# When the parts of a sequence may be added: a rule by slots, and an output bias added at the norm

## The chip, the cores and the metric

The kernel runs on one core of a Trainium2 chip. The metric is the device time of one execution in microseconds (us); a kernel's time is the median of its runs. Beside the times there is one profiled execution of each kernel, with a trace of every engine: TensorE (PE, with its weight loads as PEld), VectorE (DVE), ScalarE (ACT), GpSimd (POOL) and SyncE (SP), which here issues all plain DMAs.

## The reference: what is computed

The input x holds 16 sequences of 512 tokens with 256 features, all float32. Each token is normalised (mean and variance over its features); from the normalised tokens xn come three parts, and their sum with x is the output:

```
xn  = layernorm(x)
out = x + attention(xn) + routed(xn) + shared(xn)
attention: q, k, v = xn Wq' + bq, ...; 16 heads of 16; causal, window of 128 keys
           softmax + 1e-9, times v, then  @ Wo' + bo
routed:    logits = xn gate'; the 2 best of 8 experts (beta added for the choice),
           weight sigmoid(logit); expert: (silu(xn Wg) * (xn Wu)) Wd, width 512
shared:    one more expert of the same form for every token
```

bo is the output bias that the change moves: one vector of 256, the same for every token.

## The kernel before

**Stages.** A sequence is four tiles of 128 tokens. `norm` normalises sequences in groups of three: it loads x into the tiles `x_in` (`load_x`, two buffers per place, the next group loaded ahead), forms statistics (L211, L215) and the reciprocal root (L222 to L227) on VectorE, writes xn (L233) to memory as `xn_d`, turns it with TensorE and stores `xT_d` (L249), and makes the values v (stored as `v_d`) and the router's logits. `lane_sums` (L279, L281) adds up the values of a sequence on GpSimd, and `sum_values` (L289, L292) turns these sums with a matmul. The first sequence is normalised ahead of everything, from the tile `x_first`, the others in the background. `route` then sorts all tokens by expert. `experts` runs 135 blocks of 128 tokens, and writes their results with an indirect DMA to `y_d`. `early` is the shared expert of one sequence: it loads xT (L800), makes the hidden values (`gate_up`, L764) and adds the second product to the sum (`add_down`, L789, L794).

**Sums.** Every sequence has a running sum of 512 KB. Each of its three parts (attention, routed, shared) loads it into a tile `acc` with `load_sums`, adds its own and stores it with `store_sums` (L827), in any order but one at a time (`in_work`). The first part to come loads x itself and adds bo to it on GpSimd (L815, L816), the next load what is in memory as `acc_d` (L813), and the last part stores to the output. Attention adds its product with Wo at L777 and L780 (`output`), the routed part multiplies the two results of each token by their weights (L968) and adds them (L972) on GpSimd, in two halves per sequence, each with a y tile loaded at L990.

**Order.** The program is written out by hand in slots. The generator `attention` yields four times per step, 20 steps per sequence, 1304 slots in all. In each slot the main loop may advance the background (norms, then the router), advances the filling at an even pace (shared parts as long as the router isn't done, then all expert blocks, then the shared parts that are left), and advances the endings (routed parts, from when the last expert block is out). `now[0]` is the sequence whose attention runs. A sequence's attention is added two groups after its last scores, in slot 80 b + 101 or so. What is written out this way sets priorities: a planner with its own costs and times then puts each engine's instructions in order, and may let one go ahead of earlier ones that wait in its reckoning. On each engine and queue the order is then fixed.

**What the change touches.** `free(b)` says whether a shared or routed part of sequence b may start: nobody else is at its sum, and its attention is either not yet under way (b above `now[0]`) or has been added. `endings` takes from the free sequences those above `now[0]` first, then the lowest; `filling` takes those above `now[0]` first, and the highest.

Of the kernel before, what the change touches and what calls it, by code (L numbers as in the profile page):

```python
# [12 lines left out]
ALU = mybir.AluOpType  # L13
AX = mybir.AxisListType

B, S, D = 16, 512, 256
# [3 lines left out]
P = 128  # L20
NT = S // P
# [20 lines left out]
def block_kernel(ctx: ExitStack, tc: tile.TileContext, a: dict, out: bass.AP):  # L42
    nc = tc.nc
# [27 lines left out]
    acc_d = dram.tile([TT * P, D], FP, tag="acc_d", name="acc_d")  # L71
    y_d = dram.tile([2 * TT * P + P, D], FP, tag="y_d", name="y_d")
    by_tile = lambda d, b: d[b * S : (b + 1) * S].rearrange("(t p) d -> p t d", p=P)
# [22 lines left out]
    x_first = part_tile(0, "x_in").rearrange("p (t d) -> p t d", d=D)  # L96
# [104 lines left out]

    logits = const.tile([P, TT, E], FP, tag="logits", name="logits")

    def norm(xs, first=None):

        n = len(xs) * NT
        st = two.tile([P, NG * NT, 6], FP, tag="st", name="st")
        mv = two.tile([P, NG * NT, 2], FP, tag="mv", name="mv")
        for i, x_sb in enumerate(xs.values()):
            for t in range(NT):  # L210
                nc.vector.bn_stats(st[:, i * NT + t], x_sb[:, t])  # L211
                if t % 2:
                    yield
        for i in range(n):
            nc.vector.bn_aggr(mv[:, i], st[:, i])  # L215
        yield
        small = lambda name: two.tile([P, NG * NT], FP, tag=name, name=name)[:, :n]
        var, root, rstd, yy = small("var"), small("root"), small("rstd"), small("yy")
        nc.vector.tensor_scalar_add(var, mv[:, :n, 1], EPS)
        nc.scalar.activation(root, var, AF.Sqrt)  # L220
        yield
        nc.vector.reciprocal(rstd, root)  # L222

        nc.vector.tensor_mul(yy, rstd, rstd)
        nc.vector.tensor_mul(yy, yy, var)
        nc.vector.tensor_scalar(yy, yy, -0.5, 1.5, ALU.mult, ALU.add)
        nc.vector.tensor_mul(rstd, rstd, yy)  # L227
        yield
        for i, (b, x_sb) in enumerate(xs.items()):
            xn = two.tile([P, NT, D], FP, tag="xn", name="xn")  # L230
            for t in range(NT):
                j = i * NT + t
                nc.vector.tensor_scalar(  # L233
                    xn[:, t], x_sb[:, t], mv[:, j, 0:1], rstd[:, j : j + 1],
                    ALU.subtract, ALU.mult,
                )
                if t % 2:
                    yield
            nc.sync.dma_start(out=by_tile(xn_d, b), in_=xn)
            tag = "xT" if first else "hr"  # L240
            xT = two.tile([P, KC, S], FP, tag=tag, name="xT_new")
            for c in range(KC):
                tp = bank_a()
                for t in range(NT):
                    nc.tensor.transpose(tp[:, ts(t, P)], xn[:, t, ts(c, P)], ident)
                nc.scalar.copy(xT[:, c], tp)
            if first:
                first(xT)
            nc.sync.dma_start(out=xT_d[b], in_=xT)  # L249
            yield  # L250
            v = four.tile([P, NT, D], FP, tag="acc", name="v_new")
            for t in range(NT):
                pv = bank_b()
                for c in range(KC):
                    nc.tensor.matmul(  # L255
                        pv[:, : D + E], lhsT=xT[:, c, ts(t, P)], rhs=wv[:, c],
                        start=c == 0, stop=c == KC - 1,
                    )
                nc.vector.tensor_tensor(v[:, t], pv[:, :D], bv, ALU.add)
                nc.scalar.copy(logits[:, b * NT + t], pv[:, D : D + E])  # L260
                if t % 2:
                    yield
            nc.sync.dma_start(out=v_d[b].rearrange("(t p) n -> p t n", p=P), in_=v)
            if first:
                load_values(ws[b])
                first_xT[b] = xT
            lane_sums(v)
            yield
            if not first:
                sum_values(b)  # L270
            normed.add(b)

    vall = const.tile([P, B, KC], FP, tag="vall", name="vall")
# [9 lines left out]
    def sum_values(b):  # L283

        pall = bank_b()
        for c in range(KC):

            rows = one.tile([P, 2, QD, DK], FP, tag=f"vsum{c}", name="vsum_c")
            nc.gpsimd.tensor_copy(  # L289
                rows, vsum.rearrange("p (g c s d) -> p c s g d", c=2, s=2, d=DK)[:, c]  # L290
            )
            nc.tensor.matmul(  # L292
                pall[:, c : c + 1], lhsT=rows.rearrange("p s g d -> p (s g d)"),
                rhs=ones[:, 0:1], start=True, stop=True,
            )
        nc.scalar.mul(vall[:, b], pall[:, :KC], EVERY)
# [509 lines left out]
    in_work = set()  # L806

    def load_sums(b):
        assert b not in in_work
        in_work.add(b)  # L810
        acc = four.tile([P, NT, D], FP, tag="acc", name="acc")
        if parts_of[b]:
            nc.sync.dma_start(out=acc, in_=by_tile(acc_d, b))  # L813
            return acc
        nc.sync.dma_start(out=acc, in_=by_tile(a["x"].rearrange("b s d -> (b s) d"), b))  # L815
        nc.gpsimd.tensor_tensor(  # L816
            acc, acc, bo.unsqueeze(1).to_broadcast([P, NT, D]), ALU.add
        )
        return acc

    out_rows = out.rearrange("b s d -> (b s) d")
# [4 lines left out]
        to = out_rows if len(parts_of[b]) == 3 else acc_d  # L826
        nc.sync.dma_start(out=by_tile(to, b), in_=acc)  # L827

    def free(b):

        return b not in in_work and (b > now[0] or "attention" in parts_of[b])

    def early(b):

# [126 lines left out]
    def endings():  # L961
        added = []

        def add():
            b, half, acc, y = added.pop()
            tiles = slice(NT // 2 * half, NT // 2 * (half + 1))
            weight = prob[:, :, b * NT : (b + 1) * NT][:, :, tiles].rearrange("p k t -> p t k")
            nc.gpsimd.tensor_tensor(  # L968
                y, y, weight.unsqueeze(3).to_broadcast([P, NT // 2, 2, D]), ALU.mult
            )  # L970
            for k in range(2):
                nc.gpsimd.tensor_tensor(acc[:, tiles], acc[:, tiles], y[:, :, k], ALU.add)  # L972
            if half:
                store_sums(b, acc, "routed")

        left = set(range(B))
        while left or added:
            ready = [b for b in left if free(b)] if all_routed else []
            if not ready:
                if added:  # L980
                    add()
                yield
                continue
            b = min(ready, key=lambda b: (b <= now[0], b))
            left.remove(b)
            acc = load_sums(b)
            for half in range(2):
                y = two.tile([P, NT // 2, 2, D], FP, tag="xn", name="y_in")
                r0 = 2 * P * (b * NT + NT // 2 * half)
                nc.sync.dma_start(  # L990
                    out=y.rearrange("p t k d -> p t (k d)"),
                    in_=y_d[r0 : r0 + P * NT].rearrange("(t p k) d -> p t (k d)", p=P, k=2),
                )
                yield
                yield
                if added:
                    add()
                added.append((b, half, acc, y))
                yield
                yield  # L1000
# [7 lines left out]
    def filling():  # L1008


        b = 0
        while not routed:
            while b not in normed:
                yield None
            yield from early(b)
            b += 1
        yield from experts()
        all_routed.append(True)
        rest = set(range(b, B))
        while rest:  # L1020
            ready = [b for b in rest if free(b)]
            if not ready:
                yield None
                continue
            b = max(ready, key=lambda b: (b > now[0], b))
            rest.discard(b)
            yield from early(b)

    all_routed, now = [], [0]

    def test_maxima():

# [14 lines left out]

    for _ in norm({0: x_first}, first_projections):
        pass
    routed = []  # L1050
    behind, fill, ends = background(), filling(), endings()
    slots_in_all = 4 * (B * STEPS + len(STEP_BLOCKS) + 1)
    pace, owed = (NB * 6 + B * 24) / (slots_in_all - 4), 0.0
    for n, now[0] in enumerate(attention()):
        if not routed and n % 8 in (0, 2, 4, 6, 7):
            if next(behind, routed) is routed:
                routed.append(True)
        owed += pace
        while owed >= 1:
            owed -= 1  # L1060
            next(fill, None)
        next(ends, None)
        if n == 8:
            sum_values(0)
        if n == 4 * (B * STEPS + 1):
            again = test_maxima()
# [68 lines left out]
```

## Time and profile before

| | |
|---|---|
| median of 3 runs | 1988.27 us (1985.82 to 1989.53) |
| the profiled execution | 1989.47 us |
| its span, first to last instruction | 1987.8 us |
| mean granted clock of TensorE | 0.983 |
| busy: PE, DVE, ACT, POOL | 1916.6, 1211.1, 684.6, 605.8 us |
| DMA | 386.58 MB, mean 194 GB/s |

Times in the views are counted from the start of the span. A row of a timeline or of the chain of waits begins with its start and its length in us, then the engine, the line of the kernel and the tiles (output<-input); "SPq" is SyncE's queue, whose length is the time to issue. A row of groups gives the number of instructions, their busy time and mean length in ns, and the idle time of the engine ahead of them with what ended it. In the chain, "issue" is time in which an engine waited for nothing that the profile shows. The 40 digits of the page give the busy share of an engine in tenths, one for each fortieth of the span (49.7 us).

### The profile page before, as it was taken

The page shows a single profiled execution, that of the slowest core. Times are in us where ns is not written, and L with a number is a line of the kernel's source. Part 1 is how long each engine was busy: PE and PEld are TensorE (multiplying, and loading weights), DVE is VectorE, ACT ScalarE, POOL GpSimd, SP SyncE. Part 2 cuts the span into 40 slices and gives each one's busy share as a digit, 9 for nine tenths or more (in the row PEclk, how much of TensorE's full clock was granted, in tenths as well). Part 3 has the DMA queues.
Part 4 walks back from the last instruction along what each step waited for, and adds up shares of the span by engine and source line. Part 5 has one row for each costly group of instructions (what it writes and reads, how often), then busy time and mean ns, then how long its engine had stood idle before and what let it go on. Part 6 is the DMA issues. An engine that isn't in the chain of part 4 may idle for free.

```text
span 1987.8 us, 35311 instructions
## 1 busy us (share of the span) xinstructions
PE 1916.6 (96%) x12011; PEld 1654.5 (83%) x12011; DVE 1211.1 (61%) x3912; ACT 684.6 (34%) x1752; POOL 605.8 (30%) x765
## 2 busy tenths in 40 slices
PE   7899999999899999999999999999999999998985
PEld 4677767767789999999989899998989899985763
DVE  5767756599945565555555566555655565555652
ACT  3333323321133333333333333333333333332320
POOL 5212212210022222222222323222222222228884
PEclk9899999999999999999999999999999999999997
DMA  7634434341257676777676777777676777757774
GB/s 198 196 120 154 151 88 133 128 124 35 59 183 245 204 233 229 223 243 220 208 235 219 223 234 232 218 251 212 217 226 216 225 235 233 217 182 215 228 238 147
DMA packets 355773, 386.58 MB, mean 194 GB/s; under 512 B 118528, under 2 KB 262976, under 8 KB 355584
## 3 DMA queue, kind: packets, MB, share of 16 engines
q1 hardware_dynamic: 342624, 348.82, 55.9%
q0 software_dynamic: 12960, 35.41, 5.5%
q8 instruction: 98, 1.61, 0.3%
q14 instruction: 91, 0.75, 0.1%
HBM read 307.67 MB, written 68.09 MB: 189 GB/s over the span
## 4 chain that ended last, share of the span: by engine, by line
PE 88%; DVE 8%; POOL 1%; DMA 1%; issue 1%; ACT 0%; SPq 0%; POOLq 0%; DVEq 0%; ACTq 0%
PE a L897 24%; PE a L557 13%; PE b L915 12%; PE c L605 12%; PE a L764 9%; PE b L789 5%; PE b L777 3%; PE b L255 3%; PE a L524 2%; PE a L514 2%; PE b L887 2%; DVE hot_b L448 1%; DVE den L622 1%; DVE hot_l L444 1%; DVE probs L546 1%
## 5 line engine op out<-in xcount | busy, mean ns | idle before, releaser
L897 PE MATMUL a<-xgT,w 128*128 128x128 f32 x4320 | 548.7, 276 | 1.9 <-DVE maxima L546 1.0
L897 PEld LDWEIGHTS a<-xgT,w 128*128 128x128 f32 x4320 | 526.9, 193 | 12.7 <-issue 8.5
L550 ACT ACTIVATE probs<-probs,maxima 128x160 f32<-128x160 f32 (+4 forms) x1024 | 346.2, 401 | 528.8 <-DVE maxima L546 508.4
L546 DVE CUSTOM_DVE_ANT_0 probs<-a,window 128x160 f32<-128x160 f32 (+4 forms) x1024 | 254.1, 297 | 235.4 <-PE a L557 225.0
L605 PEld LDWEIGHTS c<-turned,spread_v 128*128 128x128 f32 x2048 | 308.9, 191 | 58.2 <-issue 42.6
L605 PE MATMUL c<-turned,spread_v 128*128 128x160 f32 (+4 forms) x2048 | 338.1, 290 | 10.5 <-DVE ctxT L623 10.1
L557 PE MATMUL a<-kT,spread 128*128 128x160 f32 (+4 forms) x2048 | 323.2, 295 | 0.0
L557 PEld LDWEIGHTS a<-kT,spread 128*128 128x128 f32 x2048 | 290.4, 192 | 33.2 <-issue 25.0
L877 POOL DMA_INDIRECT xg<-xn_d,source x135 | 132.9, 984 | 472.3 <-PE b L887 416.6
L915 PE MATMUL b<-w,hr 128*128 128x256 f32 x1080 | 271.7, 381 | 0.0
L622 DVE RECIPROCAL den<-den 64x512 f32<-64x512 f32 x64 | 214.1, 3346 | 85.3 <-ACT den L617 82.7
L764 PE MATMUL a<-xT,shared 128*128 128x512 f32 x480 | 242.0, 609 | 11.5 <-DMA xT<-xT_d 11.5
L596 DVE STREAM_TRANSPOSE turned<-probs 128x480 f32<-128x480 f32 (+1 forms) x256 | 161.8, 632 | 104.9 <-ACT probs L550 101.5
L502 POOL COPY spread_v<-v 32x256 f32<-32x256 f32 x256 | 101.4, 397 | 373.8 <-PE c L605 219.9
L922 POOL DMA_INDIRECT y_d<-y,target x135 | 132.4, 981 | 266.3 <-ACT y L921 236.5
L915 PEld LDWEIGHTS b<-w,hr 128*128 128x128 f32 x1080 | 189.8, 190 | 19.6 <-issue 2.6
L753 DVE SCALAR_TENSOR_TENSOR hr<-hr,a 128x512 f32<-128x512 f32 x135 | 91.8, 680 | 136.4 <-ACT hr L752 127.8
L789 PE MATMUL b<-shared,h 128*128 128x256 f32 x512 | 133.1, 392 | 4.4 <-DVE acc L794 2.8
L752 ACT ACTIVATE hr<-a 128x512 f32<-128x512 f32 x135 | 79.9, 592 | 149.5 <-PE a L897 142.2
L764 PEld LDWEIGHTS a<-xT,shared 128*128 128x128 f32 x480 | 83.8, 195 | 50.7 <-issue 36.1
L754 DVE SCALAR_TENSOR_TENSOR hr<-hr,a 128x512 f32<-128x512 f32 x135 | 91.8, 680 | 45.9 <-PE a L897 43.0
L789 PEld LDWEIGHTS b<-shared,h 128*128 128x128 f32 x512 | 94.4, 196 | 20.0 <-DVE acc L794 3.5
(141 smaller groups left out, 1701.1 us busy)
## 6 DMA issues: line engine op xcount, KB each, us to landing
w<-in_gp SPq DMA_DIRECT2D x135, 512.0 KB
w<-in_up SPq DMA_DIRECT2D x135, 512.0 KB
w<-in_dp SPq DMA_DIRECT2D x135, 512.0 KB
acc_d<-acc SPq DMA_DIRECT2D x32, 512.0 KB
acc<-acc_d SPq DMA_DIRECT2D x32, 512.0 KB
y_in<-y_d SPq DMA_DIRECT2D x32, 512.0 KB
xT<-xT_d SPq DMA_DIRECT2D x30, 512.0 KB
xn_d<-xn SPq DMA_DIRECT2D x16, 512.0 KB
```

Of the source, the lines that this page charges most:

```text
L546: nc.vector.tensor_tensor_reduce(out=to, in0=ps, in1=window[:, WIN - n :], scale=-SCALE, scalar=-MASKED, op0=ALU.add, op1=ALU.min, accum_o ...
L550: nc.scalar.activation(to, to, AF.Exp, bias=least, scale=-1.0)
L557: nc.tensor.matmul(ps, lhsT=spreads[group % 2][:, u].rearrange("p g q -> p (g q)"), rhs=w["kT"][:, group // 2, f:e], start=True, stop=True,)
L596: nc.vector.transpose(moved(pT, Q * blocks[0] + P * first, [[WIN, n], [P, SEEN], [1, Q]]), moved(pr, 0, [[WIN, n], [Q, SEEN], [1, Q]]),)
L605: nc.tensor.matmul(av[:, Q * k : Q * k + n], lhsT=spread_v[s][:, k], rhs=pT[:, WIN * k : WIN * k + n], start=k == ORDER[0], stop=k == ORDE ...
L622: nc.vector.reciprocal(den[mine], den[mine])
L764: nc.tensor.matmul(ps, lhsT=wt[:, c, ts(m, P)], rhs=xT[:, c], start=c == 0, stop=c == KC - 1,)
L789: nc.tensor.matmul(po[t][:, :D], lhsT=h[m][:, ts(t, P)], rhs=wd[:, m], start=m == 0, stop=m == MC - 1,)
L877: nc.gpsimd.indirect_dma_start(out=g, out_offset=None, in_=xn_d, in_offset=bass.IndirectOffsetOnAxis(ap=source[:, i : i + 1], axis=0),)
L897: nc.tensor.matmul(hidden[i][which][:, ts(m, P)], lhsT=weights[i, which][:, c, ts(m, P)], rhs=turned[i][:, c], start=c == 0, stop=c == KC - 1,
L915: nc.tensor.matmul(po[:, :D], lhsT=made[i][:, ts(m, P)], rhs=weights[i, 2][:, m], start=m == 0, stop=m == MC - 1,)
L922: nc.gpsimd.indirect_dma_start(out=y_d, out_offset=bass.IndirectOffsetOnAxis(ap=target[:, i : i + 1], axis=0), in_=y, in_offset=None,)
```

## The change

The bias is no longer added by the first part. `add_bias` adds it in place to the x tile of each sequence once its xn has been written, and the tile is stored to `acc_d` at the end of that sequence's norm. `load_sums` always loads from `acc_d`. For the first sequence both stand between its norm and the main loop. `free` no longer looks at `now[0]`: a part may start if the sequence's attention has been added, or if the present slot, plus 20 for a routed part or 40 for a shared one, lies ahead of the slot in which attention is added. The endings take sequences without their attention first.

```diff
+    def add_bias(x_sb):
+        nc.gpsimd.tensor_tensor(x_sb, x_sb, bo.unsqueeze(1).to_broadcast([P, NT, D]), ALU.add)
...
     def norm(xs, first=None):
...
             nc.sync.dma_start(out=by_tile(xn_d, b), in_=xn)
+            if not first:
+                add_bias(x_sb)
...
             if not first:
                 sum_values(b)
+                nc.sync.dma_start(out=by_tile(acc_d, b), in_=x_sb)
             normed.add(b)
...
         acc = four.tile([P, NT, D], FP, tag="acc", name="acc")
-        if parts_of[b]:
-            nc.sync.dma_start(out=acc, in_=by_tile(acc_d, b))
-            return acc
-        nc.sync.dma_start(out=acc, in_=by_tile(a["x"].rearrange("b s d -> (b s) d"), b))
-        nc.gpsimd.tensor_tensor(
-            acc, acc, bo.unsqueeze(1).to_broadcast([P, NT, D]), ALU.add
-        )
+        nc.sync.dma_start(out=acc, in_=by_tile(acc_d, b))
         return acc
...
-    def free(b):
-        return b not in in_work and (b > now[0] or "attention" in parts_of[b])
+    def free(b, slots):
+        added = 4 * ((b + 1) * STEPS + len(STEP_BLOCKS))
+        return b not in in_work and ("attention" in parts_of[b] or clock[0] + slots < added)
...
-            ready = [b for b in left if free(b)] if all_routed else []
+            ready = [b for b in left if free(b, 20)] if all_routed else []
...
-            b = min(ready, key=lambda b: (b <= now[0], b))
+            b = min(ready, key=lambda b: ("attention" in parts_of[b], b))
...
-            ready = [b for b in rest if free(b)]
+            ready = [b for b in rest if free(b, 40)]
...
     for _ in norm({0: x_first}, first_projections):
         pass
+    add_bias(x_first)
+    nc.sync.dma_start(out=by_tile(acc_d, 0), in_=x_first)
...
     for n, now[0] in enumerate(attention()):
+        clock[0] = n
```

More of the change, by code (lines that the diff above doesn't have):

```diff
@@ L1027, in filling @@
             yield from early(b)
-    all_routed, now = [], [0]
+    all_routed, now, clock = [], [0], [0]
     def test_maxima():
```

## The prediction

> **What bounds the kernel now.** I read the page first: the share of each engine and the 40 slices.
>
> ```profile
> span 1987.8 us, 35311 instructions
> PE 1916.6 (96%) x12011; PEld 1654.5 (83%) x12011; DVE 1211.1 (61%) x3912; ACT 684.6 (34%) x1752; POOL 605.8 (30%) x765
> ...
> PE   7899999999899999999999999999999999998985
> ...
> POOL 5212212210022222222222323222222222228884
> ```
>
> TensorE is busy from end to end, so work on other engines is worth something only where the PE row drops: at the start, and in the last slices, where GpSimd (POOL) rises to 8. The windows view gives PE 299.5 of 300 us busy from 1000 to 1300 us, but 74.7 of 80 from 1770, 44.3 of 50 from 1850 and 63.9 of 88 from 1900. Nothing that the change touches in the long middle can move the end; the start and the tail can.
>
> Second, the chain of waits for the tail, from 1955 us on:
>
> ```profile
> 1961.37 0.43 DVE acc L794
> ...
> 1963.33 4.57 PE b L777 x12
> ...
> 1967.92 0.10 DVE acc L780
> 1968.02 8.14 issue
> 1976.17 3.02 POOL acc L972 x3
> ...
> 1979.82 1.26 POOL acc L972
> ```
>
> The last matmul (L777, attention's output of sequence 15) ends at 1967.9. Then 8.14 us pass in which no engine works, and GpSimd adds the routed results of sequence 15. SyncE's timeline says what the 8.14 us are:
>
> ```profile
> 1961.82 0.47 SPq L827 DMA_DIRECT2D out<-acc  x1
> 1968.38 0.37 SPq L827 DMA_DIRECT2D acc_d<-acc  x1
> 1972.11 0.37 SPq L813 DMA_DIRECT2D acc<-acc_d  x1
> 1981.11 0.38 SPq L827 DMA_DIRECT2D out<-acc  x1
> ```
>
> The sum of sequence 15 goes to acc_d (3.73 us until the next DMA may read it), comes back (4.06 us until L972 starts at 1976.17), takes 4 adds (4.92 us) and is stored at 1981.11; 6.7 us later the span ends. The two y tiles were already weighted (L968, until 1968.0), so nothing else holds the end.
>
> Third, the same view at the start, and GpSimd's bias add by form:
>
> ```profile
> 22.95 0.68 POOL vsum L279
> ...
> 25.29 0.30 POOL vsum_c L289
> 25.59 0.04 issue
> 25.64 0.61 PE b L292 x4
> 26.25 0.75 PE a L557 x6
> ```
>
> ```profile
> L816 POOL TENSOR_TENSOR acc<-acc,bo 128x1024 f32<-128x1024 f32 x16 | 37.7, 2355 | 24.1 <-DMA acc<-in_x 15.3 <-issue 8.1
> ```
>
> Until 25.6 us the chain runs through GpSimd: fills, then vsum and vsum_c, which the first PE work after the projections (L292) waits for, with the first scores (L557) behind it.
>
> **Part by part. Which part comes last.** I counted slots through the loops: 1304 slots, 24 steps of filling per shared part, 8 slots per routed part, the experts done at slot 1170. Before, sequences 14 and 15 wait for their attention (slots 1221 and 1301), so the routed part of 15 starts at 1302 and must follow attention 15 through acc_d. After, 14 is let in at 1170 and 15 at 1202 (the limits are 1200 and 1280). But the shared part of 11, in both versions the last of the filling, holds 11 from slot 1274 to 1301, so the routed part of 11 becomes the last one. The round trip is not removed: it now follows the shared part of 11 and lies beside attention 15, whose sum goes straight to the output.
>
> Its length from the rows above: the shared part's last add (L794) ends at 1961.8; store 3.7 gives 1965.5; load 4.1 gives 1969.6; 4 adds of 4.9 give 1974.5, against 1981.1: a gain of 6.6 us. What is late next is attention 15: its store leaves at 1968.4, and with the same 6.7 us behind it would end the span at 1975.1, earlier than 1974.5 + 6.7 = 1981.2, so it is covered. The lower bound: if the load of 11 or its second y tile is queued on SyncE behind attention 15's output store, it leaves at 1968.8, lands at 1972.9, and the adds end at 1977.8: a gain of 3.3. I take 6.4, near the upper end, since the load depends only on a store issued 6.6 us before that output store, and let 0.2 go for its issue.
>
> **Bias at the norm.** 16 adds on GpSimd before, 16 after, at 2.355 us: no change in sum. Fifteen follow the writing of xn; one, for sequence 0, stands ahead of the first scores. The fifteen lie under PE work: from 120 to 420 us PE is busy 296.6 of 300 us. What is queued behind such an add is spread_v (L502) and vsum. Taken out of the tail is one add (at 1854.5); GpSimd then waits 4.56 us for y_in anyway at 1863.99, so I book nothing.
>
> The add of sequence 0 comes, by program order, between L281 and L289: vsum_c, L292 and L557 move by up to 2.4 us. On the other side, if the planner puts the scores ahead of L292, they wait only for the spread DMAs, the last of which is issued by 21.0; with 3.7 us for landing (a 512 KB row, theirs are 32 KB) that is 24.7 instead of 26.25, a gain of 1.5. Ends: -1.5 and +2.4. I take +1.2: the row is on the chain, but from 42.5 to 58.1 us the chain lies on VectorE, with statistics that don't depend on the first scores and could absorb half.
>
> **Stores and loads.** 16 more stores of 512 KB (L827 issues take 0.37 us: 6 us of SyncE over the first 400 us), and 16 loads read acc_d in place of x. That is 8.4 of 386.6 MB, in stages where the DMA engines are 0.35 to 0.67 busy: cost 0, hidden behind PE. If SyncE waits for an add, behind it queue the spreads (L494) and the loads of v and xT; but SyncE's own waits already reach 13.4 us (L494 for PE) in a run whose PE is 96% busy. The buffers of x are held until their store lands; groups are loaded one group ahead, except the first, which is the rival below.
>
> **A lock between two engines.** One row speaks against adds on GpSimd beside the norms. The chain, then GpSimd's timeline:
>
> ```profile
> 158.16 2.34 DVE yy L225
> ```
>
> ```profile
> 158.11 2.35 POOL L816 TENSOR_TENSOR acc<-acc,bo 128x1024 f32<-128x1024 f32 x1
> ```
>
> The small product L225, 0.15 us elsewhere, took exactly as long as the bias add beside it, and stood on the chain. So one collision costs up to 2.2 us, and the fifteen adds now follow the norm's own steps. Per group of three there are three products with two inputs in SBUF (L224, L225, L227), 15 in all; one was hit before. I expect none to two after: -2.2 to +2.2, booked at 0. The Trainium skill, "SBUF — State Buffer", section "Who interferes with whom", states that such a VectorE instruction and a GpSimd one that reads SBUF block each other for the whole instruction. By that rule alone, with a hit in each of the 5 groups, the sum would be about 9 us worse than mine (four hits more than now, 2.2 us each). The L233 rows (median 0.41 us), one SBUF tensor and scalars, show no such stretch beyond 0.82 us.
>
> On the round trip the skill speaks too: "DMA: Bandwidth & Descriptors", section "Anatomy of one DMA", puts about 2.0 us of fixed cost on each DMA, most of it the receipt of the last byte, so by its fit store and load would be some 6.4 us (estimate: 2 x (2.0 + 1.2)). The rows show 7.79, and go into the sum.
>
> **The sum.** -6.4 (tail) + 1.2 (start) + 0 + 0 = -5.2 us. The profiled execution took 1989.47 us, its span 1987.8; that gives 1984.3 for such a run. The median is 1.2 lower, 1988.27, and the forecast is made from it: 1988.27 - 5.2 = 1983.1 us, 0.26% faster. About 0.2%, or 4 us, is what a measurement of this kernel can tell from no change. The likeliest case's own range: tail -3.3 to -6.6, start -1.5 to +2.4, so 1980.2 to 1987.4.
>
> **The rivals.**
>
> *The start takes it back: slower.* The first group of x tiles reuses the buffer of sequence 0's x. It is now free only when that sequence's store has landed: vsum done 25.25, add 2.36, store 3.73, load of x for sequence 1 4.1 to 5.3 (y_in at 1960.77 landed at 1966.1): 35.4 to 36.6. Its first statistics (L211) ran at 29.3. If VectorE's order keeps them there, VectorE stands for up to 7.3 us with the scores' maxima (L546) behind, and PE behind these. With +2.4 and only 3.3 gained in the tail: +6.4, 1994.7 us. It decides from a wait of about 5 us on. For it: L211 already waited 4.3 us in all for x, and PE is 12.7 us idle in the first 60. Against: the statistics were already strewn from 29 to 50 us, and xn only followed at 50.8.
>
> *The gain is lost on the way: no change.* Tail -3.3, start +2.4: -0.9, 1987.4. For it: SyncE runs strictly in order, and it waited for GpSimd or VectorE at nearly every store of the tail. Against: the dependency of the load ends 2.9 us before attention 15's store.
>
> *The order shuffles a load of xT: a larger gain.* Two waits of PE are of one kind, a shared part's xT issued right behind the store of the last one:
>
> ```profile
> 67.82 5.50 DMA xT<-xT_d
> ```
>
> ```profile
> 1893.20 5.97 DMA xT<-xT_d
> ```
>
> Other xT loads (1846.9, 1917.9) were issued early enough. Since routed parts change places on SyncE, the second wait may go: -5.2 - 6.0 = -11.2, 1977.1. As well could another come; then +0.8, in the case of no change.
>
> **How the numbers follow.** The forecast case gets 0.50: 0.40 of it beyond 4 us of gain, 0.10 within. Lost on the way 0.14, slower 0.30, larger gain 0.06. So faster 0.46, within 0.2% 0.24, slower 0.30. The range reaches from a larger gain with the start at its lower end (-6.4 - 1.5 - 6.0 = -13.9, 1974.4, rounded to 1975.0) to the slower case with the spread of the runs above the median, 1.3, against it (1994.7 + 1.3, cut to 1995.5). Some 0.2 stays outside, for other shuffles of the order.
>
> **What would show it.** In the profile after: the last GpSimd adds belong to sequence 11 and start near 1969 to 1973; the gap named issue ahead of them shrinks from 8.14 to under 5; two output stores stand last on SyncE, 5 to 9 us apart. At the start, a bias add stands between L281 and L289 and L557 begins near 27 to 28.6. L211 waiting for x_in by over 4 us early on means the slower rival. A last matmul outside 1964 to 1972 means that a step I booked at 0 carried the result.

## The result: slower by 0.38%, and the profile after

The changed kernel took 1994.75 us (median of 7 runs, 1993.66 to 1996.6) beside 1988.27 us before: a ratio of 1.0038 (95% interval 1.0026 to 1.0049), some 7.5 us slower (the medians are 6.5 us apart). The profiled execution took 1993.66 us with a span of 1991.9. The forecast was 1983.1 us and faster; the rival named "slower" stood at 1994.7.

The page of the changed kernel, its span, shares, and the slices of TensorE and GpSimd:

```profile
span 1991.9 us, 35343 instructions
PE 1919.7 (96%) x12011; PEld 1656.7 (83%) x12011; DVE 1215.8 (61%) x3912; ACT 684.4 (34%) x1752; POOL 605.4 (30%) x765
...
PE   7799999999999999999999999999999999998985
...
POOL 5322213110022222222222222222222222228784
```

The shares are those of before. All of GpSimd's bias adds now lie in the first sixth of its slices; before, five of the 16 lay beyond 1100 us. Where the time lies is seen by following one row through both traces. I took the reciprocal of the softmax sums (L622 before, L629 after, 64 of them in the same sequence): the changed kernel's are later by 3.2 us at the first one, 9.2 at the second (123 us), 8.5 to 8.7 from 303 to 760 us, 5.7 at the last one, and the span ends 4.1 later. So in these two executions time is lost before 303 us, and the tail, from the last reciprocal to the end, gains 1.6.

**The start.** The chain of waits of the changed kernel from 22 to 32 us; L206 is the moved bias add:

```profile
22.70 0.04 POOL x_in L206
22.73 2.26 issue
24.99 0.72 POOL vsum L286
...
27.72 1.01 PE b L299 x4
28.73 2.45 PE a L564 x10
```

The add stands ahead of the value sums, even of the first one, and L299 starts at 27.72 instead of 25.64: 2.1 us. Then VectorE's timeline, first the kernel before, then the changed one with TensorE's wait beside it:

```profile
50.80 1.76 DVE L233 TENSOR_SCALAR xn<-x_in,mv,rstd 128x256 f32<-128x256 f32 x5
...
54.20 3.33 DVE L622 RECIPROCAL den<-den 64x512 f32<-64x512 f32 x1
```

```profile
57.37 3.34 DVE L629 RECIPROCAL den<-den 64x512 f32<-64x512 f32 x1 [0.51 <-ACT den L624]
60.64 1.27 DVE L237 TENSOR_SCALAR xn<-x_in,mv,rstd 128x256 f32<-128x256 f32 x4
```

```profile
61.00 2.19 PE L251 MATMUL a<-ident,xn 128*128 128x128 f32 x8 [4.44 <-DVE xn L237]
```

Before, xn of sequence 1 came first (50.80) and the reciprocal after it (54.20). Now 3.34 us of reciprocal stand ahead of xn, and TensorE sits idle for 4.44 us until 61.00. The lock of which the prediction spoke shows too, here on the chain, with GpSimd's timeline beside it:

```profile
74.23 2.10 DVE var L223
```

```profile
73.96 2.34 POOL L206 TENSOR_TENSOR x_in<-x_in,bo 128x1024 f32<-128x1024 f32 x1
```

And a wait that the prediction confined to the first group of x comes at the last one (chain, 180 to 260 us, then GpSimd's and TensorE's timelines):

```profile
215.47 6.89 DMA acc_d<-x_in
222.37 4.32 DMA x_in<-in_x
...
232.41 2.35 DVE var L223
```

```profile
232.36 2.35 POOL L206 TENSOR_TENSOR x_in<-x_in,bo 128x1024 f32<-128x1024 f32 x1 [9.61 <-DVE mv L219]
```

```profile
237.64 3.50 PE L261 MATMUL b<-wv,xT_new 128*128 128x264 f32 x8 [2.01 <-ACT logits L266]
```

A load of x waits 6.9 us for the store from its buffer, the statistics wait for the load, and then var (0.08 us where the chain of the run with the rule alone has one, at 69 us) is blocked by an add again. TensorE stands idle for 2.01 us, and its next eight matmuls take 3.50 us; eight of the same line took 1.78 us at 181 us.

**The tail.** The chain, SyncE's timeline with one row of the kernel before ahead of it, and GpSimd's timeline:

```profile
1967.79 6.27 DMA acc_d<-acc
1974.48 5.36 DMA acc<-acc_d
1979.96 0.44 DVE acc L787
1980.44 3.80 PE b L784 x8
```

```profile
1939.76 1.46 SPq L813 DMA_DIRECT2D acc<-acc_d  x3
```

```profile
1967.79 0.97 SPq L828 DMA_DIRECT2D acc_d<-acc  x1
1974.08 0.91 SPq L819 DMA_DIRECT2D acc<-acc_d  x2
1983.10 2.00 SPq L828 DMA_DIRECT2D out<-acc  x2
```

```profile
1978.14 4.93 POOL L974 TENSOR_TENSOR acc<-acc,y_in 128x512 f32<-128x512 f32 x4 [3.61 <-DMA acc<-acc_d]
```

The L819 row has two loads, by the count of slots in the prediction that of sequence 11 for its routed part, which waits for the store, and right behind it that of sequence 15 for its attention, which depends on nothing of the kind. Before, the latter was among the three issued near 1940. Attention's product (L784) therefore ends at 1984.2 instead of 1967.9: the wait for acc_d, which had come after the last matmuls, now comes ahead of the last eight of them.

### The profile page after: what moved, and what is told of

Its sections match the earlier page's. It is cut to its first block, busy times and chain, and to the rows that moved or that the text cites. A ratio compares the mean times of both kernels' runs of the same rounds, so it can differ in the third digit from the quotient of the medians.

```text
span 1991.9 us, 35343 instructions
## 1 busy us (share of the span) xinstructions
PE 1919.7 (96%) x12011; PEld 1656.7 (83%) x12011; DVE 1215.8 (61%) x3912; ACT 684.4 (34%) x1752; POOL 605.4 (30%) x765
## 4 chain that ended last, share of the span: by engine, by line
PE 88%; DVE 7%; issue 2%; DMA 2%; ACT 0%; POOL 0%; SPq 0%; DVEq 0%; POOLq 0%; ACTq 0%
PE a L899 24%; PE a L564 13%; PE c L612 12%; PE b L917 12%; PE a L771 9%; PE b L796 5%; PE b L784 3%; PE b L261 3%; PE a L521 3%; PE a L531 3%; PE b L889 2%; DVE hot_b L455 1%; DVE den L629 1%; DVE hot_l L451 1%; PE a L251 1%
## 5 line engine op out<-in xcount | busy, mean ns | idle before, releaser
L629 DVE RECIPROCAL den<-den 64x512 f32<-64x512 f32 x64 | 214.1, 3346 | 84.0 <-ACT den L624 81.4
```

Source lines behind the costliest of these rows:

```text
L629: nc.vector.reciprocal(den[mine], den[mine])
```

## The experiments

Nine kernels; L numbers are those of each kernel. The trace of each gives one execution, and the ratio comes from 4 to 11 runs beside 11 to 21 of the kernel before (medians 1986.7 to 1988.2); 0.001 is 2.0 us.

### The rule alone, and the norm alone

```diff
 # rule alone: the kernel before, with
-        return b not in in_work and (b > now[0] or "attention" in parts_of[b])
+        added = 4 * ((b + 1) * STEPS + len(STEP_BLOCKS))
+        return b not in in_work and ("attention" in parts_of[b] or clock[0] + slots < added)
...
-            b = min(ready, key=lambda b: (b <= now[0], b))
+            b = min(ready, key=lambda b: ("attention" in parts_of[b], b))
 # norm alone: the changed kernel, with these lines the other way round
```

> The kernel before with the new rule alone: free by slots, the endings' new order; the bias is added by the first part as before, and nothing is stored at the norm. Theory A (three places: the bias add and store of sequence 0 cost 8.7 us at the start, the adds missing from GpSimd later give back 2.9, the tail gains 1.6): start and middle stand as before (reciprocals of L622 within 0.3 us up to 1700 us), the tail gains 1 to 3 us, span 1985 to 1987, about 0.1% faster. Rival B (the new order of parts itself costs time in the tail, which the trace hides under the shift): span 1989 or more.

Measured: 0.9984 (0.9972 to 0.9996), 3.2 us faster, span 1983.5.

> The changed kernel with the old rule and the old orders of choice: bias and store at the norm alone. Theory A: +8.7 us by 520 us, back to +5.7 by 1750, tail as before: span 1993 to 1994.5, 0.25 to 0.35% slower than before. Rival B (the cost comes from the rule): as before, 1988.

Measured: 1.0046 (1.0032 to 1.0061), 9 us slower, span 1994.6. The two halves of the change go in opposite directions, and their sum (+0.30%) is near the whole (+0.38%). The rule gains, the norm loses. B falls on both sides.

One part of theory A falls too. In the trace of the rule alone, TensorE, VectorE and ScalarE have exactly the order of the kernel before, and yet its reciprocals come 1.7 us late at 303 us and 1.4 us early at 1598. The 2.9 us that "came back in the middle" of the changed kernel are therefore no effect of the missing adds: the profiled execution of the kernel before was slow there. Shifts of 2 to 4 us between single executions mean nothing by themselves; the ratios decide.

### Sequence 0 as before

```diff
-    add_bias(x_first)
-    nc.sync.dma_start(out=by_tile(acc_d, 0), in_=x_first)
...
+        if b == 0 and not parts_of[b]:
+            nc.sync.dma_start(out=acc, in_=by_tile(a["x"].rearrange("b s d -> (b s) d"), b))
+            add_bias(acc)
+            return acc
         nc.sync.dma_start(out=acc, in_=by_tile(acc_d, b))
```

> The changed kernel, but sequence 0 is treated as in the kernel before: nothing is added or stored ahead of the main loop, and its first part loads x and adds the bias. The other fifteen keep add and store at the norm. Theory A (sequence 0 alone costs the start): at the reciprocals the shift against before is within 2 us up to 520 us, about -3 by 1750, and the span 1982 to 1984.5, 0.2 to 0.3% faster than before. Rival C (the fifteen adds and stores in the norms cost the start): shift of +5 or more by 520 us, span 1990 or more. Rival D (the 2.9 us that came back in the middle are slack that a late start used up, not the adds that are gone from GpSimd): no shift in the middle, span 1986 to 1987.5.

Measured: 1.0011 (1.0002 to 1.0020), 2.2 us slower, span 1986.1. Against the changed kernel that is 5.4 us gained, so sequence 0 costs about 5; but against the rule alone the other fifteen still cost 0.27%, also about 5 us. A, which laid everything on sequence 0, and C, which laid it on the fifteen, are each half right. The trace shows a part of what the fifteen cost. The chain of this kernel, then GpSimd's timeline, and last the same five instructions on the chain of the run without the fifteen adds (below):

```profile
54.05 4.07 DVE xn L237 x5
```

```profile
55.64 2.33 POOL L206 TENSOR_TENSOR x_in<-x_in,bo 128x1024 f32<-128x1024 f32 x1
```

```profile
54.31 1.77 DVE xn L237 x5
```

Five xn took 4.07 us instead of 1.77, because one of them stood still during a bias add. In all, VectorE's instructions beside the adds were stretched by 5.2 us here and 5.6 in the changed kernel, against 2.2 before (each one's length less the median of its form).

### The store, the add

```diff
 # store, no add: the changed kernel, without
-    add_bias(x_first)
 # add, no store: sequence 0 as before, and ahead of the main loop
+    add_bias(x_first)
```

> The changed kernel without the bias add of sequence 0 ahead of the main loop (so that sequence 0 lacks the output bias); its x is still stored to acc_d there. What is left is the store, and x of sequence 1 queued behind it. Theory A1 (two costs: the add ahead of the value sums delays the first scores by 2 us and costs clock, some 4.8 us by 50 us; the queued x moves the reciprocal L629 ahead of xn, some 4.6 us more): vsum ends near 25.3, first scores near 26.5, xn of sequence 1 near 55 to 56, shift of about +4 by 520 us, span 1987 to 1989. Rival F (all of it is the add): shift 0, span 1983 to 1984. Rival G (all of it is the queued x): shift +8.7, span 1992.

Measured: 1.0027 (1.0018 to 1.0037), 3.2 us above the kernel with sequence 0 as before. Its profiled execution (span 1985.1) was the quickest of ten, so the span expected does not decide. VectorE's order has the reciprocal ahead of xn, as in the changed kernel: the store alone brings that about.

> The kernel with sequence 0 treated as before, with one bias add more: on the x tile of sequence 0 ahead of the main loop, unused by anything. The value sums wait for the add as in the changed kernel, but nothing is stored there, and xn stands ahead of the reciprocal on VectorE again. Theory A1: first scores near 28.5 us, matmuls after a longer idle time of PE at half the clock for some 3 us, then +4.8 us against before until xn of sequence 1; shift of +3 to +5 by 520 us, span 1987 to 1989. Rival F (all is the add): shift +8.7, span 1992. Rival G (all is the queued x): shift 0, span 1983 to 1984.

Measured: 1.0020 (1.0010 to 1.0030), 1.8 us above, span 1989.8, first scores at 29.2 us, xn ahead of the reciprocal again. So by the medians both count, the store with what it reorders about 3 us, the add about 2, together 5.0 of the 5.4, and neither F nor G holds. But the intervals overlap: only the sum of the two is firm, and G, in which the add costs nothing, is not excluded by the times alone.

### The fifteen without their adds

```diff
             nc.sync.dma_start(out=by_tile(xn_d, b), in_=xn)
-            if not first:
-                add_bias(x_sb)
```

> Sequence 0 as in the kernel before, the other fifteen x tiles stored at their norm, but without the bias add on GpSimd (so that these fifteen sequences lack the output bias). It tells the adds from the stores in what the fifteen cost (1.0011 with both, 0.9984 with the rule alone). Theory H (GpSimd's adds block VectorE's xn and var, 2.7 us on the chain before 73 us; the stores are hidden): no L237 above 0.9 us beside others of 0.41, span near that of the rule alone, ratio to before 0.998 to 0.9995. Rival I (the fifteen stores and what queues behind them on SyncE cost it): ratio 1.0005 to 1.002.

Measured: 0.9969 (0.9958 to 0.9980), 6.2 us faster than before, span 1979.5. H is right in its direction and too small: without the adds the fifteen stores cost nothing that shows, and the adds cost 0.42%, 8.3 us, at the norm. Taking them out also changed the planner's order: 124 of VectorE's 3912 places, between 116 and 233 us, hold another instruction, so a part of the 8.3 us may be order. At their old place the fifteen, less what the stores cost, come to about 3 us (0.9984 against 0.9969, with intervals that overlap). In this trace no wait for x is on the chain from 130 to 420 us, and TensorE is busy 380.7 us of the 390 from 30 to 420, against 377.4 in the kernel with sequence 0 as before.

The reciprocals say where. By the second one (123 us) the kernel with sequence 0 as before is 2.6 us behind this run, with xn and var blocked on its chain and no wait for x there. Between the fourth and the fifth one (194 to 232 us) each of the seven kernels that have the adds at the norm loses 4.1 to 4.2 us more, and neither this run nor the two with the adds at their old place and the new rule loses anything: this is where the load of x is late, var is blocked, and TensorE idles for 2.0 us. How much of these 4.1 us is the lock and how much the late store of x (it can leave only when the add is done) was not told apart. The 3 us at the old place have a spot too, in TensorE's timeline of the kernel before:

```profile
292.59 0.61 PE L292 MATMUL b<-ones,vsum_c 128*128 128x1 f32 x4 [1.69 <-POOL vsum_c L289]
```

A bias add of 2.36 us, from 288.34, stood ahead of the value sums there. Here that wait is 0.35 us, and the reciprocals come 3.0 us earlier between 261 and 303 us, as they do in every kernel with the stores at the norm.

### Attention 15's sum loaded ahead

```diff
+            if i == (n_groups + 1) * n_steps - 2:
+                ahead[B - 1] = load_sums(B - 1)
...
-        acc = load_sums(b)
+        acc = ahead.pop(b, None) or load_sums(b)
```

> The changed kernel with the sum of sequence 15 loaded for its attention some 9 slots earlier, ahead of the load for the routed part of 11 that waits for a store. Theory A (attention 15 stood behind that load): PE's last matmuls (L784) end near 1974 in place of 1984, one output store leaves near 1974.5, the last adds of 11 on GpSimd end near 1983 as now, and the span falls by 1.5 to 2.5 us to about 1990: the round trip of 11 is then the end. Rival (the attention's sum alone was the end): span 1982.

Measured: 1.0031 (1.0019 to 1.0042), 1.4 us below the changed kernel, which the intervals don't separate. The trace (the quickest of seven executions) does, from the last reciprocal on. SyncE's timeline:

```profile
1966.05 0.37 SPq L831 DMA_DIRECT2D acc_d<-acc  x1
1971.18 0.36 SPq L822 DMA_DIRECT2D acc<-acc_d  x1
1972.53 8.36 SPq L831 DMA_DIRECT2D out<-acc  x2
```

One load waits now, attention's store leaves at 1972.5 and the last matmul ends at 1972.0. From the last reciprocal to the end of the span it is 24.7 us, against 28.2 in the changed kernel, 27.2 with the rule alone and 29.8 before: that is 3.4 us less than in the changed kernel, of which 1.2 lie in the store (5.08 us until it can be read instead of 6.27), and 2.5 less than with the rule alone. So the queue behind that load was worth some 2 to 2.5 us of these, and the round trip of 11 is the end.

### No round trip at the end

```diff
-            b = min(ready, key=lambda b: ("attention" in parts_of[b], b))
+            b = min(ready, key=lambda b: ("attention" in parts_of[b], "shared" in parts_of[b], b))
```

This order puts the routed parts of sequences whose shared part is still to come (11 among them) first, so that shared part and attention are the last ones and store to the output. It was run with sequence 0 as before, and with the rule alone.

> As the run with sequence 0 as before, and the endings take sequences whose shared part is still missing ahead of the others, so that the routed part of 11 is added before its shared part and nothing goes through memory at the end. Theory A (the end is the round trip through acc_d, and attention 15's load queued behind it): the last matmul as before less 3 us, then one output store and 6.7 us: span 1971 to 1974, 0.7 to 0.85% faster than before. Rival E (GpSimd's adds set the tail, whatever the order): the last adds end near 1976 and the span is 1980 or more.

Measured: 0.9945 (0.9932 to 0.9957), 10.9 us faster than before and 13.1 faster than the same kernel without the order; span 1973.1. The chain at its end, and SyncE's timeline:

```profile
1961.83 4.34 PE b L784 x12
1966.17 0.02 issue
1966.19 0.42 DVE acc L787
```

```profile
1961.76 5.26 SPq L832 DMA_DIRECT2D out<-acc  x3
```

Nothing is loaded after the last matmul; the last of three output stores leaves at 1966.65. From the last reciprocal to the end it is 16.6 us. The last GpSimd add ends at 1961.7, so E, GpSimd as the limit of the tail, falls.

> The kernel before with the new rule and with sequences whose shared part is missing taken first by the endings; the bias stays with the first part, nothing is stored at the norm. If costs add up (rule alone -3 us, order of the endings -13 us): span 1969 to 1973, ratio to before 0.991 to 0.993, the fastest of all. If the bias adds of late first parts weigh on GpSimd in the tail: no better than 0.9945.

Measured: 0.9939 (0.9925 to 0.9952), 12.0 us faster than before (1976.22 beside 1988.18 us), span 1970.9. It is the fastest kernel of the study, 16.7 us from the last reciprocal to the end, but short of the 0.991 to 0.993 expected, and not clearly faster than the one before it: of the 5 us that the fifteen had cost, the times show about 1 here. Whether the cost depends on the rest of the order, or the intervals (each some 2.5 us to either side) hide it, stays open.

## Why the prediction was wrong, step by step

**The tail: the round trip foreseen, the queue behind its load not.** The last adds do wait for a round trip behind the last shared part, as counted. The term was -6.4 us (ends -3.3 and -6.6). The trace shows -1.6, the rule alone -3.2 by its times and -2.6 by its trace. Two things were mis-sized. The failing step is "What is late next is attention 15": it took the load of attention 15's sum for as early as before, and asked what is queued on SyncE behind attention's store, not what is queued behind the waiting load. That was worth some 2 to 2.5 us. And the store took 6.27 us to be readable, not 3.73, with two other transfers issued in the 1.0 us ahead of it. The fit for one DMA that the prediction quotes from the Trainium skill, "DMA: Bandwidth & Descriptors", section "Anatomy of one DMA", is given there for GpSimd's path; these transfers are SyncE's, and the sum did not use it.

**The start: +1.2 booked, about +5 measured.** The add ahead of the value sums was priced rightly at its upper end (2.1 us in the trace against 2.4; 1.8 in the times, not clear of noise), and by these half of it should not have been forgiven. The store ahead of the first load of x was named, but only as a rival: about 3 us. It did not act as that rival said. VectorE did not stand waiting for x (its statistics simply came later), but the planner, presumably because x was late in its reckoning, put a reciprocal of 3.34 us ahead of xn.

**Bias at the norm, and the lock: 0 booked, about 5 measured** against the rule alone (8.3 at the new place less 3 at the old), and the largest error. The row on which it rested was the right one, a VectorE instruction as long as the add beside it. But the step counted only products with two inputs in SBUF, and took L233 for safe because its longest instance was 0.82 us in a trace in which no add lay beside an xn. The blocked ones were xn and var, each with one tensor as input. The Trainium skill, "SBUF — State Buffer", section "Who interferes with whom", says that `tensor_scalar` too can take both ports in one of its modes and then excludes GpSimd; L237 (2.79 us in place of 0.41) and L223 (2.34 in place of 0.15) agree with that, and the prediction had used only half of the section's list.

**The loads of x.** "Groups are loaded one group ahead" was true and did not help at the last group: 6.9 us for the store and 4.3 for the load were on the chain at 215 us, ahead of the blocked var and TensorE's 2.0 us.

**The rivals.** "Slower" gave 1994.7 against 1994.75 measured. That is a coincidence in its terms: it had 7.3 us from one wait for x, where the runs show three smaller costs (add, store with its reordering, lock). "Lost on the way" was half right on the tail. No xT load changed its kind: the second wait was 5.97 us before and 6.20 after.

## What to carry to other kernels

A part moved out of the last place can stay in the way through the queue: when a load has to wait for a store, look at every load that stands behind it, and let the parts that may store straight to the output be the last ones. Work moved to an engine "with room" must be checked against what runs beside it at the new place, instruction by instruction; one row in which a small instruction takes exactly as long as its neighbour is a warning for all of its kind. And where a planner orders the engines, a tile that comes later can put an unrelated long instruction ahead of the short one that matters.

## What the runs showed of the hardware

**The granted clock at the start differs from one execution to the next.** The windows view from 24 to 34 us, the kernel before and then the rule alone, which has the same order on TensorE; the last three columns are granted clock, DMA share and GB/s:

```profile
24.00:34.00 10.00, 8.37 (x34) 5.20 (x35) 6.38 (x31) 5.03 (x12) 3.21 (x9) 1.00 1.09 240
```

```profile
24.00:34.00 10.00, 7.97 (x23) 5.43 (x24) 3.42 (x19) 3.49 (x8) 4.19 (x11) 0.66 1.14 257
```

A clock of 1.00 in one and 0.66 in the other, and 34 matmuls instead of 23. The Trainium skill, "TensorE: Matmul & The Clock Gate", section "What's actually happening", describes a free-running window that decides on the clock, so that the ramp varies between runs of one kernel; the two rows agree with that. A clock of 0.66, as the changed kernel has in this window too, is therefore no proof that the add lowered it. Whether the add makes it likelier stays open: the four executions with it ahead of the value sums show 0.57 to 0.67, the seven without it 0.66 to 1.00.

**A bias add can hold a small VectorE instruction for nearly its whole length.** `var` over 128x12 elements (0.15 us elsewhere) took 2.34 us beside an add of 2.35 us in the changed kernel, and xn over 128x256 (0.41 us) took 2.79 beside one of 2.33 in the kernel with sequence 0 as before. Not every instruction is held: in the latter trace a reciprocal beside an add of 2.35 us, at 59.8 us, took 3.33 us as it does elsewhere, and sums from TensorE's results (L265, L801) kept their 0.42 us.
